# Layer 3: the 3x3 convolution of the last 32 channels moved from TensorE to ScalarE and GpSimd

## The chip, the cores and the metric

The kernel runs on one core of a Trainium2 chip. The metric is the device time of one execution, in microseconds (us); the figure for a kernel is the median of its runs. A profiled execution gives the trace that the views below are taken from. In them, PE is TensorE, DVE is VectorE, ACT is ScalarE, POOL is GpSimd, and SP is the engine that issues most DMAs.

## What is computed

Four layers run one after another on x, four images of 48 channels and 256 x 256 pixels in float32. Each adds its result to its input, which it first normalises over groups of channels. Layer 0 is a gated network with a depthwise 3x3 convolution and an 8x8 frequency filter, layers 1 and 2 are scans with a convolution along rows and columns, and layer 3, which the change touches, is this (shortened):

```python
y = jnp.einsum('oc,bchw->bohw', w_in, x)               # 48 -> 288 channels
yp = ...                                               # 8 x 8 patches of y
f = jnp.fft.rfft2(yp) * fft_mask[None]
yp = jnp.fft.irfft2(f, s=(P, P))
y = lax.conv_general_dilated(y, w_dw, ..., feature_group_count=288)   # 3x3, each channel by itself
x1, x2 = jnp.split(y, 2, axis=1)                       # 144 and 144 channels
g = jax.nn.gelu(x1, approximate=False) * x2
return jnp.einsum('oc,bchw->bohw', w_out, g)           # 144 -> 48 channels
```

## The kernel before

Images are worked on in two pairs. In layer 3 (`layer3`) each pair is cut into 32 strips of 8 rows (`RB`); a strip and one tail row at the end of the pair make 33 steps, 66 in all. The 3x3 convolution needs the rows above and below, so a step's convolved rows lie one row higher than its strip, and `lines` copies the last two rows of the strip before on ScalarE.

One step goes as follows. `fetch` brings a strip from memory (a DMA on SP's queue). `ready` normalises it into the tile `u` (eight ACTIVATEs, line 1043). `turn` transposes it on TensorE (line 1058), `wave` takes it to the frequency domain (line 1072), `spectra` applies the 48 to 288 matrix (line 1093), and DVE applies the mask while it copies the result out of PSUM (lines 1096 and 1101). `pixels` brings four blocks of channels back to pixels (line 1131); ACT and DVE copy them out (line 1051; letters such as "AD" say which engine takes which half) into the tiles `z_a0`, `z_a1`, `z_b0`, `z_b1`. The 144 channels of each half of the network are 128 and 16. a0 and b0 hold the first 128 of x1 for the first and the second image, a1 and b1 the first 128 of x2. The remaining 16 channels of each half, 32 in all, of both images make the fifth group, m: `pixels_rest` (line 1150) brings it to `z_m`, 64 partitions at a time, the upper and the lower half of the partitions in turn for odd and even steps.

The convolution is done in two ways. On TensorE, `taps` (line 1167) and `lower_taps` (line 1183) do nine products with a diagonal 32 x 32 matrix for each block of 32 channels and two rows, accumulated in PSUM. On DVE, `begin` makes the first product on ACT (line 1222) and queues eight taps (line 1227, a scalar times a shifted tile plus the accumulator, all in SBUF) in the list `due`; these do the upper four rows of b0 and b1. A final gelu on ACT (line 1229) and a product on DVE (line 1231) close them.

TensorE's share is cut into units, run two at a time in `together`, one for each lane: lane l does blocks 2l and 2l+1, and the taps of both lanes alternate. There are units a0 and a1 for both lanes, b (the lower four rows of b0 and b1) for both lanes, and m for one lane a step. Two steps make fourteen units, that is seven rounds of `together`. During a round `together` also takes five items from `due`. After a unit its result leaves PSUM: a0 by a gelu on ACT (`curve`, line 1204), a1 by a product on DVE (`gate`, line 1210), b by a gelu on ACT and a product on DVE (lines 1193 and 1194), m by both (lines 1204 and 1210) into `g_m`.

`store` drains what is left in `due` for a step and calls `mixed`: the projection from 144 to 48 channels on TensorE (lines 1249 and 1259), into two PSUM tiles `po`; DVE adds the strip of the input (line 1272), and SP writes it out. Its last products read `g_m`.

Layer 3 is scheduled by hand: each engine's queue holds its instructions in the order in which the program writes them, within the loop at the end of `layer3`, which writes two steps per pass. PSUM has four tiles of two banks (`ps_w`) for everything, taken in turn.

Of the kernel before, what the change touches and what calls it, by code (L numbers as in the profile page):

```python
# [33 lines left out]
class Net:  # L34
# [901 lines left out]
    def layer3(self, x, scs):  # L936
# [11 lines left out]
        with ExitStack() as st:  # L948
# [54 lines left out]
            for half in range(2):  # L1003
                lo = half * HD
                nc.sync.dma_start(wd[:, half, :], self.a["L3_w_dw"][lo : lo + NM, :])
                for l in range(2):
                    at = 64 * l + 32 * half
                    nc.sync.dma_start(wd[at : at + 2 * NR, 2, :], self.a["L3_w_dw_r"][half])
            diag = wp.tile([128, 3, 9, 32], F32, name="diag")
            none = wp.tile([128, 1], F32, name="none")  # L1010
            nc.gpsimd.memset(none, 0.0)

# [14 lines left out]

            zt = {}
            for g in ("a0", "a1", "b0", "b1", "m"):
                zt[g] = (wz if g == "m" else wp).tile([128, RB + 2, WP], F32, name=f"z_{g}", tag=f"z_{g}")  # L1030
                nc.gpsimd.memset(zt[g][:, :, 0:1], 0.0)
                nc.gpsimd.memset(zt[g][:, :, WP - 1 : WP], 0.0)
            gated = {g: wz.tile([128, 4, MM], F32, name=f"g_{g}", tag=f"g_{g}") for g in "ab"}
            gated["m"] = wz.tile([128, 1, MM], F32, name="g_m", tag="g_m")

# [69 lines left out]

            def lines(step, g):

                n, at, old = (64, 64 * odd(step), 64 - 64 * odd(step)) if g == "m" else (128, 0, 0)  # L1110
                t, above = zt[g][at : at + n], zt[g][old : old + n]
                if step[1] == 0:
                    nc.gpsimd.memset(t[:, 0:2, 1 : W + 1], 0.0)
                else:
                    nc.scalar.copy(t[:, 0:2, 1 : W + 1], above[:, RB : RB + 2, 1 : W + 1])
                if tail(step):
                    nc.gpsimd.memset(t[:, 2, 1 : W + 1], 0.0)
                return t
# [22 lines left out]
            def pixels_rest(step, eng):  # L1141

                t = lines(step, "m")
                if tail(step):
                    return
                pp = ps_w.tile([128, 2, 8, 64], F32, name="pp", tag="w")
                for q in range(NQ):
                    for l in range(2):
                        f = slice(64 * l, 64 * l + 64)
                        nc.tensor.matmul(  # L1150
                            pp[64 * (q % 2) : 64 * (q % 2) + 64, l, q // 2, :],
                            zr[f, q, :], self.inv1[f, :], start=True, stop=True,
                        )
                to = t[:, 2 : RB + 2, 1 : W + 1].rearrange("p h (q j l w) -> p j l q h w", j=2, l=2, w=8)
                for j in range(2):
                    for l in range(2):
                        copy(eng[l], to[:, j, l], pp[64 * j : 64 * j + 64, l].rearrange("p q (h w) -> p q h w", w=8))

            def taps(step, g, half, blocks, pd):
                for t in range(9):
                    for j in range(1 if tail(step) else 4):
                        n = 1 if tail(step) else R2
                        for i, k in enumerate(blocks):
                            s = slice(32 * k, 32 * k + 32)
                            nc.tensor.matmul(  # L1167
                                pd[32 * j : 32 * j + 32, i, 0:n, :], diag[s, 2 if g == "m" else half, t, :],
                                zt[g][s, R2 * j + t // 3 : R2 * j + t // 3 + n, t % 3 : t % 3 + W],
                                start=(t == 0), stop=(t == 8),  # L1170
                            )
                    yield True
# [43 lines left out]
            def begin(step, half):  # L1216
# [16 lines left out]

                due.extend(((step, half), lambda t=t: tap(t)) for t in range(1, 9))

            def drain(step, half):

                while any(key == (step, half) for key, _ in due):
                    due.pop(0)[1]()

            def mixed(step):
# [2 lines left out]
                h0 = s * RB - 1  # L1244
                js, n = (range(1), 1) if tail(step) else (range(4), R2)
                pos = [ps_w.tile([128, 2, R2, W], F32, name="po", tag="w") for _ in js[::2]]
                part = whole.pop(step)
                for j in js[:2]:
                    nc.tensor.matmul(  # L1249
                        pos[0][64:128, j, 0:n, :], wo_b, part[:, R2 * j : R2 * j + n, :], start=True, stop=False  # L1250
# [1 line left out]
                for i in range(5):  # L1252
                    for j in js:
                        for b in range(2):
                            if b and j < 2 and i < 4:
                                continue
                            r = slice(32 * j, 32 * j + 32)
                            src = gated["m"][r, 0] if i == 4 else gated["ab"[b]][r, i]
                            nc.tensor.matmul(  # L1259
                                pos[j // 2][64 * b : 64 * b + 64, j % 2, 0:n, :], wo[r, i + b * (i == 4), :],  # L1260
                                src[:, 0 : n * W].rearrange("p (r w) -> p r w", w=W),
                                start=(i == 0), stop=(i == 4),
                            )
                for j0, po in zip(js[::2], pos):
# [20 lines left out]
            out, units = set(), [[], []]  # L1285
            for n, step in enumerate(steps):
                for l in range(2):
                    units[l] += [(step, img) for img in ("a0", "a1", "b") + (("m",) if n % 2 == l else ())]
            assert len(units[0]) == len(units[1])
            waiting = [None, None]  # L1290

            def unit(l, step, img):
# [4 lines left out]
                if img == "b":  # L1297
                    if not tail(step):
                        pd = ps_w.tile([128, 2, R2, W], F32, name="pd", tag="w")
                        yield from lower_taps(step, blocks, pd)  # L1300
                else:
                    pd = ps_w.tile([128, 2, R2, W], F32, name="pd", tag="w")
                    half = int(img[1]) if img[0] == "a" else 0
                    yield from taps(step, img, half, blocks, pd)
                if img == "a0":
                    waiting[l] = curve(step, pd)
                    return
                assert n == 0 or steps[n - 1] in out
                if img == "a1":
                    gate(step, "a", 2 * l, waiting[l], pd)  # L1310
                elif img == "m":
                    gate(step, img, 0, curve(step, pd[:, 0:1]), pd[:, 1:2])
                elif pd is not None:
                    lower_gate(2 * l, pd)

            def together(k, aside=None):


                going = [unit(l, *units[l][k]) for l in range(2)]
                for t in range(9):  # L1320
                    for g in list(going):
                        if next(g, None) is None:
                            going.remove(g)
                    if t == 1 and aside is not None:
                        aside()
                    if due and (t + 1) * 5 // 9 > t * 5 // 9:
                        due.pop(0)[1]()
                for g in going:
                    assert next(g, None) is None
# [38 lines left out]
            def lower(n, half, q0, eng):  # L1368
# [3 lines left out]
                if q0:  # L1372
                    begin(steps[n], half)

            fetch(steps[1])
            scale(1)
            ready(0)
            turn(0, "AD")
            wave(0, "AD")
            spectra(0, 0)  # L1380
            for k in range(3):
                for t in range(9):
                    nc.vector.tensor_scalar(diag[:, k, t, :], eye, wd[:, k, t : t + 1], None, ALU.mult)
            ready(1)
            k = 0
            for n in range(0, S, 2):
                o = n + 1
                pixels(steps[n], "a0", 0, "AD")
                pixels(steps[n], "a0", 8, "AD")
                spectra(n, 1, slice(0, 2))  # L1390
                lower(n, 0, 0, "AA")
                spectra(n, 1, slice(2, 4))
                lower(n, 0, 8, "AA")
                spectra(n, 1, slice(4, None))
                together(k)

                pixels(steps[n], "a1", 0, "DD")
                pixels(steps[n], "a1", 8, "DD")
                store(n - 1)
                if fresh(n + 2):  # L1400
                    fetch(steps[n + 2])
                turn(o, "AA")
                together(k + 1)

                wave(o, "AA")
                lower(n, 1, 0, "AA")
                lower(n, 1, 8, "AA")
                spectra(o, 0)
                together(k + 2)

                pixels(steps[o], "a0", 0, "AD")
                pixels(steps[o], "a0", 8, "AD")
                pixels_rest(steps[n], "AD")
                spectra(o, 1, slice(0, 3))
                lower(o, 0, 0, "AA")
                spectra(o, 1, slice(3, None))
                together(k + 3)

                pixels(steps[o], "a1", 0, "DD")
                pixels(steps[o], "a1", 8, "AD")  # L1420
                store(n)
                if fresh(n + 3):
                    fetch(steps[n + 3])
                lower(o, 0, 8, "AA")
                together(k + 4, lambda: ready(n + 2))

                turn(n + 2, "AA")
                lower(o, 1, 0, "DD")
                lower(o, 1, 8, "AD")
                wave(n + 2, "A", (0,))  # L1430
                together(k + 5)

                pixels_rest(steps[o], "AD")
                wave(n + 2, "A", (8,))
                spectra(n + 2, 0)
                together(k + 6, lambda: ready(n + 3))
                k += 7
            store(S - 1)


# [116 lines left out]
```

## Time and profile before

| | |
|---|---|
| median of 3 runs | 12905.28 us (12900.96 to 12907.49) |
| profiled execution | 12935.81 us, span 12934.0 us |
| layer 3 in the span | from about 8560 us to the end, some 4370 us |
| busy in the whole span | PE 94%, DVE 58%, ACT 28%, POOL 10% |
| mean granted TensorE clock | 0.985 of full speed |
| tap matmuls of layer 3 in the trace | z_a 37152 records, z_b 18432, z_m 9288 (two records for each matmul) |

Lines of the trace give a start in us from the span's start, a length in us, the engine, the line of the kernel, the operation, the tile written and the tiles read, and the shape (partitions x elements). "x4" is a run of four such instructions merged. Square brackets hold the idle time of the engine just before, and what ended it. In a table by stretch each engine's entry is its busy time and, in brackets, its instructions; the last three columns are the granted clock, the DMA share and GB/s. A matmul's end is modelled, so matmuls that run beside each other in different parts of the array each show some 0.6 us, while a round of 288 records takes 9.75 us.

### The profile page before, as it was taken

The numbers are of one execution on the slowest core, as the hardware profiler recorded it, in microseconds if no ns is written. First come the engines' busy times: TensorE is split into PE (matmuls) and PEld (weight loads), VectorE is DVE, ScalarE is ACT, GpSimd is POOL, SyncE is SP. The second block draws the span as 40 slices with busy tenths as digits, with TensorE's granted clock in tenths as the row PEclk, the third lists the DMA queues.
The fourth block names the chain that finished last, engine by engine and source line by source line (L and its number), as shares of the span: only waits on it lengthen the run. The fifth ranks groups of instructions, "written<-read, shape, count | busy, mean of one in ns | idle before, by whom it ended". The sixth has DMA issues, their size and how long they took to land.

```text
span 12934.0 us, 426071 instructions
## 1 busy us (share of the span) xinstructions
PE 12148.3 (94%) x199864; PEld 7975.0 (62%) x199864; DVE 7459.6 (58%) x11269; ACT 3608.4 (28%) x4015; POOL 1333.8 (10%) x977
## 2 busy tenths in 40 slices
PE   2999999999999999999999999989999999999999
PEld 0333333335777777777777777766666666666666
DVE  6777777774333334663333335566666666676666
ACT  1444444442223200002233000023333333333333
POOL 0010010100000001540000004510000000000000
PEclk9999999999999999999999999999999999999999
DMA  7222222225765776987756877931111111111111
GB/s 176 56 56 56 56 58 56 58 53 96 155 138 152 172 155 134 225 199 157 145 144 155 173 153 178 229 61 28 23 28 28 28 26 26 28 23 28 28 28 21
DMA packets 1170350, 1224.62 MB, mean 95 GB/s; under 512 B 1027668, under 2 KB 1031756, under 8 KB 1107724
## 3 DMA queue, kind: packets, MB, share of 16 engines
q1 hardware_dynamic: 1066052, 623.85, 26.2%
q0 software_dynamic: 87488, 445.55, 11.9%
q10 hardware_dynamic: 15048, 127.96, 5.4%
q8 instruction: 1566, 25.66, 0.9%
q14 instruction: 196, 1.61, 0.0%
HBM read 699.79 MB, written 497.42 MB: 93 GB/s over the span
## 4 chain that ended last, share of the span: by engine, by line
PE 87%; ACT 5%; DVE 3%; issue 3%; DMA 2%; SPq 0%; POOL 0%; ACTq 0%; DVEq 0%; POOLq 0%
PE acc L682 40%; PE pd L1167 12%; PE pd L313 9%; PE pd L1183 5%; PE pp L1131 4%; PE pz L1093 4%; PE po L1259 2%; PE ph L290 2%; PE ph L282 1%; DMA gx<-in_x 1%; PE py L387 1%; PE po L457 1%; PE py L394 1%; PE po L1249 1%; PE pf L1072 1%
## 5 line engine op out<-in xcount | busy, mean ns | idle before, releaser
L682 PE MATMUL acc<-line,w_down 96*96 96x256 f32 x12240 | 2660.9, 379 | 14.5 <-ACT line L780 4.9
L682 PEld LDWEIGHTS acc<-line,w_down 96*96 96x96 f32 x12240 | 1989.1, 163 | 671.5 <-DVE line L824 11.5
L1167 PE MATMUL pd<-z_a,diag 32*32 32x512 f32 x37152 | 1622.2, 596 | 42.2 <-issue 32.3
L313 PE MATMUL pd<-main,diag 32*32 32x512 f32 x36864 | 1426.8, 622 | 66.6 <-issue 63.6
L682 PE MATMUL acc<-line,w_right 96*96 96x256 f32 x6120 | 1339.9, 380 | 23.4 <-DVE line L862 18.2
L1227 DVE SCALAR_TENSOR_TENSOR acc<-z_b,wd,acc 128x1024 f32<-128x1024 f32 (+1 forms) x1056 | 1326.1, 1258 | 60.8 <-ACT acc L1222 33.5
L682 PE MATMUL acc<-line,w_left 96*96 96x256 f32 x6120 | 1339.2, 379 | 9.6 <-DVE line L903 7.6
L350 DVE SCALAR_TENSOR_TENSOR acc<-rest,wd,acc 128x1024 f32<-128x1024 f32 x1024 | 1256.7, 1285 | 127.2 <-ACT acc L344 127.0
L682 PEld LDWEIGHTS acc<-line,w_right 96*96 96x96 f32 x6120 | 997.1, 163 | 354.4 <-DVE line L862 19.0
L682 PEld LDWEIGHTS acc<-line,w_left 96*96 96x96 f32 x6120 | 996.0, 163 | 339.0 <-DVE line L903 16.1
L1167 PEld LDWEIGHTS pd<-z_a,diag 32*32 32x32 f32 x37152 | 857.4, 103 | 524.3 <-issue 233.2
L313 PEld LDWEIGHTS pd<-main,diag 32*32 32x32 f32 x36864 | 505.0, 105 | 779.8 <-issue 666.6
L865 DVE SCALAR_TENSOR_TENSOR line<-acc,b_right,in 96x256 f32<-96x256 f32 x1020 | 489.6, 480 | 850.7 <-PE acc L682 850.7
L789 DVE TENSOR_TENSOR line<-acc,in 96x256 f32<-96x256 f32 x1020 | 428.9, 421 | 920.2 <-PE acc L682 914.3
L824 DVE SCALAR_TENSOR_TENSOR line<-acc,b_down,in 96x256 f32<-96x256 f32 x992 | 476.1, 480 | 830.3 <-PE acc L682 823.5
L1183 PE MATMUL pd<-z_b,diag 32*32 32x512 f32 x18432 | 933.0, 597 | 2.6 <-issue 1.9
L903 DVE SCALAR_TENSOR_TENSOR line<-acc,b_left,in 96x256 f32<-96x256 f32 x992 | 475.8, 480 | 530.9 <-PE acc L682 530.9
L124 ACT ACTIVATE nrm<-nrm 96x2 f32<-96x2 f32 (+1 forms) x7 | 1.4, 203 | 2796.2 <-DVE nrm L123 1421.9
L913 POOL TENSOR_TENSOR blk<-blk,line 96x1024 f32<-96x1024 f32 x248 | 705.3, 2872 | 608.1 <-DVE line L903 608.1
L1096 DVE TENSOR_TENSOR z<-pz,mask 128x768 f32<-128x768 f32 (+2 forms) x640 | 627.5, 1003 | 218.4 <-PE pz L1093 215.8
L831 ACT COPY blk<-line 96x1024 f32<-96x1024 f32 (+2 forms) x264 | 479.7, 1888 | 922.9 <-DVE line L824 760.6
L1131 PEld LDWEIGHTS pp<-c_inv,z 64*64 64x64 f32 x32768 | 528.9, 136 | 252.3 <-issue 140.9
(167 smaller groups left out, 12915.3 us busy)
## 6 DMA issues: line engine op xcount, KB each, us to landing
blk<-x ACTq DMA_DIRECT2D x64, 1536.0 KB, 18.1
in<-x SPq DMA_DIRECT2D x248, 384.0 KB, 11.2
dn<-line POOLq DMA_DIRECT2D x124, 768.0 KB, 9.5
rt<-line POOLq DMA_DIRECT2D x124, 768.0 KB, 9.9
in<-rt SPq DMA_DIRECT2D x124, 768.0 KB, 12.8
in<-dn SPq DMA_DIRECT2D x120, 768.0 KB, 6.9
in<-up SPq DMA_DIRECT2D x240, 384.0 KB, 11.7
up<-blk POOLq DMA_DIRECT2D x56, 1536.0 KB, 14.5
```

The costliest lines, as they stand in the source:

```text
L313: nc.tensor.matmul(pd[32 * j : 32 * j + 32, i], diag[s, t, :], z[s, R2 * j + t // 3 : R2 * j + t // 3 + R2, t % 3 : t % 3 + W], start=(t = ...
L350: nc.vector.scalar_tensor_tensor(to, at(t, r), wd[:, 1, t : t + 1], to, ALU.mult, ALU.add)
L682: self.nc.tensor.matmul(acc, w[:, t, :], carry[:, :, t : t + m], start=(t == 0), stop=(t == 2))
L831: nc.scalar.copy(blk[:, :, e, lo:hi, k // 2 : k // 2 + RH], inner(ln[:, e::2])[..., lo:hi].rearrange("p h i w -> p i w h"),)
L865: nc.vector.scalar_tensor_tensor(blocks(inner(line)), blocks(acc), br, new, ALU.add, ALU.add)
L913: (nc.vector if w0 == 0 else nc.gpsimd).tensor_tensor(part, part, inner(ln[:, f::2])[..., lo:hi].rearrange("p w i h -> p i h w"), ALU.add)
L1093: nc.tensor.matmul(pz[:, b, q, :], xf[s, q0 + q, :], wi[s, NM * k : NM * k + m], start=True, stop=True)
L1096: nc.vector.tensor_tensor(zs[k][:, q0 : q0 + n].rearrange("p q b c -> p b q c"), pz[:, :, :, 0:NM], mask[:, :, :, NM * k : NM * k + NM].to ...
L1131: nc.tensor.matmul(pp[64 * c : 64 * c + 64, l, q, :], z[f, q0 + q, b, 64 * c : 64 * c + 64], self.inv1[f, :], start=True, stop=True,)
L1167: nc.tensor.matmul(pd[32 * j : 32 * j + 32, i, 0:n, :], diag[s, 2 if g == "m" else half, t, :], zt[g][s, R2 * j + t // 3 : R2 * j + t // 3 ...
L1183: nc.tensor.matmul(pd[to, i], diag[s, half, t, :], zt[f"b{half}"][s, R2 * j + t // 3 : R2 * j + t // 3 + R2, t % 3 : t % 3 + W], start=(t ...
L1227: nc.vector.scalar_tensor_tensor(acc, at(t), wd[:, half, t : t + 1], acc, ALU.mult, ALU.add)
```

## The change

The m units are taken out of TensorE. `z_m` is now split by rows instead of by steps: partitions 0 to 63 hold the strip's upper part and partitions 64 to 127 the lower, so that all 128 partitions each give four convolved rows. `pixels_rest` therefore writes four pieces of four rows and four of six rows.

`narrow` queues 18 products in the list `coming`: nine taps by two halves of two rows. A product is one ACTIVATE on ScalarE that multiplies a shifted view of `z_m` by the channel's weight. For the first tap it writes the accumulator `acc_m`; for the others it writes the tile `part`, which has two buffers, and GpSimd adds `part` to `acc_m`. `together` calls `product` at given taps: seven times in the round of a1, seven in the round of b, four in the round of a0 of the next step. `ready` stands in the round of b, at its fifth tap. `gate_few` is called at the seventh tap of that a0 round: it issues what is left of the products, and `narrow_gate`, two gelus on ScalarE and four products on VectorE. `mixed` reads the result from `acc_m` instead of `g_m`.

The loop now writes one step per pass, with three rounds of `together`, and six items of `due` are taken in a round. `diag` has two groups instead of three. Cut to its core:

```diff
@@ lines
-                n, at, old = (64, 64 * odd(step), 64 - 64 * odd(step)) if g == "m" else (128, 0, 0)
-                t, above = zt[g][at : at + n], zt[g][old : old + n]
+                t = zt[g]
+                t, last = (t, t[:, RB:]) if g != "m" else (t[0:64], t[64:128, HR:])
@@ pixels_rest
-                to = t[:, 2 : RB + 2, 1 : W + 1].rearrange("p h (q j l w) -> p j l q h w", j=2, l=2, w=8)
-                for j in range(2):
-                    for l in range(2):
-                        copy(eng[l], to[:, j, l], pp[64 * j : 64 * j + 64, l].rearrange("p q (h w) -> p q h w", w=8))
+                for h0, h1, lo, to in ((0, HR, 2, t), (HR - 2, RB, 0, zt["m"][64:128])):
+                    to = to[:, lo : HR + 2, 1 : W + 1].rearrange("p h (q j l w) -> p j l q h w", j=2, l=2, w=8)
+                    for j in range(2):
+                        for l in range(2):
+                            copy(
+                                eng[l], to[:, j, l],
+                                pp[64 * j : 64 * j + 64, l].rearrange("p q (h w) -> p q h w", w=8)[:, :, h0:h1],
+                            )
+            def narrow(step):
+                n, rows = (64, 1) if tail(step) else (128, HR)
+                at = lambda t: zt["m"][0:n, t // 3 : t // 3 + rows, t % 3 : t % 3 + W]
+                acc = mid.tile([128, HR, W], F32, name="acc_m", tag="acc_m")
+                few[step] = acc
+                acc = acc[0:n, 0:rows]
+                half = lambda ap, r: ap[:, R2 * r : min(R2 * r + R2, rows)]
+                def tap(t, r):
+                    if t == 0:
+                        nc.scalar.activation(half(acc, r), half(at(0), r), AF.Identity, bias=none[0:n], scale=wd[0:n, 2, 0:1])
+                        return
+                    part = mid.tile([128, R2, W], F32, name="part", tag="part", bufs=2)[0:n, 0 : min(R2, rows)]
+                    nc.scalar.activation(part, half(at(t), r), AF.Identity, bias=none[0:n], scale=wd[0:n, 2, t : t + 1])
+                    nc.gpsimd.tensor_tensor(half(acc, r), half(acc, r), part, ALU.add)
+                halves = range(1 if tail(step) else 2)
+                coming.extend(lambda t=t, r=r: tap(t, r) for t in range(9) for r in halves)
+            def product(last=False):
+                while coming:
+                    coming.pop(0)()
+                    if not last:
+                        return
+            def narrow_gate(step):
+                gl, acc = io.tile([128, HR, W], F32, name="gl", tag="gl"), few[step]
+                for j0 in (0,) if tail(step) else (0, 2):
+                    x1, x2 = slice(32 * j0, 32 * j0 + 32), slice(32 * j0 + 32, 32 * j0 + 64)
+                    rows = 1 if tail(step) else HR
+                    nc.scalar.activation(gl[x2, 0:rows], acc[x1, 0:rows], AF.Gelu)
+                    for j in range(1 if tail(step) else 2):
+                        to, r = slice(32 * (j0 + j), 32 * (j0 + j) + 32), slice(R2 * j, min(R2 * j + R2, rows))
+                        nc.vector.tensor_tensor(acc[to, r], gl[x2, r], acc[x2, r], ALU.mult)
@@ units and together
-                    units[l] += [(step, img) for img in ("a0", "a1", "b") + (("m",) if n % 2 == l else ())]
+                    units[l] += [(step, img) for img in ("a0", "a1", "b")]
-                    if t == 1 and aside is not None:
-                        aside()
-                    if due and (t + 1) * 5 // 9 > t * 5 // 9:
+                    if t in aside:
+                        aside[t]()
+                    if due and (t + 1) * 6 // 9 > t * 6 // 9:
                         due.pop(0)[1]()
@@ the loop, one step per pass (the two-step pass of before is in the listing above)
+            def gate_few(n):
+                if n >= 0:
+                    product(True)
+                    narrow_gate(steps[n])
+            for n, step in enumerate(steps):
+                pixels(step, "a0", 0, "AD")
+                pixels(step, "a0", 8, "AD")
                 spectra(n, 1, slice(0, 2))
                 lower(n, 0, 0, "AA")
                 spectra(n, 1, slice(2, 4))
                 lower(n, 0, 8, "AA")
                 spectra(n, 1, slice(4, None))
+                together(3 * n, {t: product for t in range(4)} | {6: lambda: gate_few(n - 1)})
+                pixels(step, "a1", 0, "DD")
+                pixels(step, "a1", 8, "AD")
+                pixels_rest(step, "AD")
                 store(n - 1)
+                narrow(step)
                 if fresh(n + 2):
                     fetch(steps[n + 2])
+                turn(n + 1, "AA")
+                together(3 * n + 1, {t: product for t in range(2, 9)})
+                wave(n + 1, "AA")
                 lower(n, 1, 0, "AA")
                 lower(n, 1, 8, "AA")
+                spectra(n + 1, 0)
+                together(3 * n + 2, {t: product for t in range(8) if t != 4} | {4: lambda: ready(n + 2)})
+            gate_few(S - 1)
             store(S - 1)
```

## The prediction

> **What bounds the kernel now.** I read the page's busy slices and its chain first: layer 3 is the last third, from 8560 us on, and the chain runs on TensorE (PE) nearly throughout. Then busy time by stretch:
>
> ```profile
> core 0: us, PE busy (x) PEld busy (x) DVE busy (x) ACT busy (x) POOL busy (x), PEclk, DMA share, GB/s
> 8700.00:12750.00 4050.00, 3839.25 (x114165) 2622.74 (x114166) 2754.20 (x3277) 1480.43 (x2134) 4.19 (x10) 0.99 0.15 27
> ```
>
> PE is busy 95%, VectorE (DVE) 68%, ScalarE (ACT) 37%, GpSimd (POOL) never. The waits of PE in layer 3 say how rarely it is held: mostly by nothing the profile shows, and only some tens of us by copies. So the stage lasts as long as PE's list. Next the chain in order of time, for one step:
>
> ```profile
> 9625.02 9.68 PE pd L1167 x272
> 9634.70 2.02 PE pp L1131 x128
> 9636.72 1.86 PE po L1249 x4
> 9638.58 4.50 PE po L1259 x62
> ```
>
> One round of `together` (two lanes, 288 matmul records) takes 9.75 us; 4370 us of layer 3 (8560 to the end) over 64 full steps and two short ones make 66.5 us a step (3.5 rounds, and transforms between), 62 without half a round. Then the order of DVE and ACT in that step, since the change lives in their queues (start, length, engine, line):
>
> ```profile
> 9625.01 1.24 ACT L1222 ACTIVATE acc<-z_b,none,wd 128x1024 f32<-128x1024 f32 x1
> 9634.40 1.94 ACT L1204 ACTIVATE gl<-pd 128x1024 f32<-128x1024 f32 x2 [8.15 <-PE pd L1167]
> 9626.40 1.27 DVE L1227 SCALAR_TENSOR_TENSOR acc<-z_b,wd,acc 128x1024 f32<-128x1024 f32 x1
> 9627.71 1.22 DVE L1231 TENSOR_TENSOR acc<-acc,acc 128x1024 f32<-128x1024 f32 x1
> 9628.85 5.24 DVE L1227 SCALAR_TENSOR_TENSOR acc<-z_b,wd,acc 128x1024 f32<-128x1024 f32 x4
> 9636.88 2.48 DVE L1051 COPY z_a<-pp 128x512 f32<-128x512 f32 x4 [2.79 <-ACT z_a L1115]
> ```
>
> ACT idles 8 us in a round: room for products. DVE fills the same round with `tap` instructions back to back, 1.20 us apart, both tensor operands in SBUF. Would POOL additions run beside them? Layers 0 to 2 show both engines together:
>
> ```profile
> 278.11 7.25 DVE L350 SCALAR_TENSOR_TENSOR acc<-rest,wd,acc 128x1024 f32<-128x1024 f32 x6
> 280.04 5.80 POOL L274 COPY rest<-rest 128x512 f32<-128x512 f32 x1 [10.11 <-ACT rest L296]
> 296.69 1.87 POOL L274 COPY main<-main 128x1024 f32<-128x1024 f32 x1 [10.86 <-PE pd L313]
> 297.69 1.95 DVE L350 SCALAR_TENSOR_TENSOR acc<-rest,wd,acc 128x1024 f32<-128x1024 f32 x1
> 5743.13 5.67 POOL L913 TENSOR_TENSOR blk<-blk,line 96x1024 f32<-96x1024 f32 x2 [8.11 <-DVE line L903]
> 5746.16 2.76 DVE L913 TENSOR_TENSOR blk<-blk,line 96x64 f32<-96x64 f32 x1
> ```
>
> The POOL copy (median 0.62) took 5.80: it sat until the whole train of DVE taps was over. The DVE sum of 96x64 (0.25 at its least) took 2.76: it sat until the POOL sum ended. Either blocks the other when both read two SBUF operands (a POOL copy too). The 541 DVE instructions of line 903 beside POOL sums, which read PSUM and SBUF, kept their 0.48 us.
>
> **Part by part, per step** (64 full steps, 2 tails).
>
> *Removed.* The m units: 72 matmuls of 32x512 (two records each; 9288 in all), half a round: 9.75/2 = -4.9 us of PE, on the path. Their gelu (0.60 ACT) and gate (0.69 DVE) go too, and nine `diag` instructions once, hidden. Order and PSUM tiles of the other units stay; each step now has the list of the former even steps, plus `pixels_rest` ahead of `store`.
>
> *Rest copies.* Four of 64x512 (0.65 ACT, 0.69 DVE, each waiting for the last, 2.7 us in all) become eight of 256 or 384 columns, about 8 x 0.5 = 4 us. They lie beside the output projection (1.86 + 4.50 us): nothing; without that cover 1.3.
>
> *Products.* 18 ACTIVATEs of 128x512. Rows: 112x256 at 0.588, 128x1024 at 1.231, so 0.80 each, 0.75 apart: 13.5 us. Two gelus of 32x1024 at 1.01 (row of 64x1024). ACT gets from 25 to some 41 us of 62: fits in sum.
>
> *Additions.* 16 on POOL, 128x512. Nearest row 96x1024 at 2.87; the two copy forms (1.045 and 0.616) give 0.19 fixed; (2.87 - 0.19)/2 + 0.19 = 1.52 us, 24 us a step. Bounds: 1.43 (half the row) and 2.87. The Trainium skill, "GPSIMD Engine Reference", Performance versus the Vector engine, gives 4497 ns for such a sum of 2048 columns; a quarter is an estimate of 1.12 us, and with it the stalls below would shrink by some 3 us a step, to about 13,120.
>
> *The port.* DVE needs it for 16 taps x 1.2, one product 1.2 and four narrow gates x 0.6 = 23 us, POOL 24: 47 of 62 us. In sum it fits; the order decides. `part` has two buffers, so ACT's third product waits for POOL's first addition, and behind ACT's product stand its gelus out of PSUM, whose four tiles hold PE. Times below run from the first tap matmul of a round.
>
> Round a0 (four products, then `narrow_gate` in the middle of DVE's taps). ACT's first product ends at 2.0. DVE starts taps at 1.4. Before the narrow gelus the port must serve four additions (6.1); DVE's four taps and one product ahead of the narrow gates take 6.0. If POOL gets in after two taps (at the 0.04 us gap ahead of L1231, as at 296.69), additions end at 10.0, the gelus at 12.0, DVE's rest at 13.6, its gates and two last taps at 18.4. If DVE's train goes first (as at 280.04), additions end at 13.5, gelus at 15.5, DVE at 19.1. Before, DVE was at its a1 copies at 11.9 (the row at 9636.88). These now end at 19.8 to 20.5; the second `po` tile needs their PSUM, wanted at 9.7 + 2.1 + 1.2 + 1.9 = 14.9. Stall 4.9 to 5.6; I take 5.0. Without the lock: 0.3.
>
> Round a1 (seven products, five additions; four taps). DVE's taps end near 5, the additions near 12.5, the last product near 10.3; wanted by then are only DVE's gates (one operand in PSUM) and ACT's copies at 11. Nothing. If this cover goes, 4.
>
> Round b (seven products and additions; six taps; `ready`, eight ACTIVATEs of 0.59, after the fourth product). ACT starts at -1.5, after L1222. Two additions end at 2.3; then a train of six taps (7.2) and further additions take turns. Whichever is first, additions three to five and the taps end at 2.3 + 7.2 + 4.6 = 14.1, and only then has product seven a buffer: it ends at 14.9, the first lower gelu at 15.9, its gate on DVE at 17.1 where it was at 11.7 (9676.27 + 1.2). PE wants that tile for the next spectra: stall about 5; 4.5 taken, as PE has two pixel groups ahead. Without the lock, product seven ends at 9.9: 0.2.
>
> *Clock.* PE's granted clock after an idle window:
>
> ```profile
> 9389.72:9393.12 3.40, 1.48 (x98) 1.34 (x94) 0.00 (x0) 2.70 (x4) 0.00 (x0) 1.00 0.02 5
> 9393.14:9396.54 3.40, 3.40 (x66) 3.28 (x58) 0.26 (x1) 2.23 (x3) 0.00 (x0) 0.50 0.02 5
> ```
>
> 1.9 us idle in 3.4 brought 3.4 us at half clock, 1.7 us of work lost. Two stalls per step: 0 to 3.4; I take one, 1.7, since after round b PE runs beside a DVE-bound stretch. The Trainium skill, "TensorE: Matmul & The Clock Gate", Why this matters for your kernels, asks for idle gaps over about 3 us; this row shows 1.9 enough, and by the page the stalls, broken by short groups, would often cost nothing here, some 110 us less.
>
> `fetch` now comes every step, one round and a half ahead of `ready`; it lands in 7.7 us and has some 24 (a round of 9.75, the 10 us up to the next, four taps of 1.1). SP carries the same transfers, POOL has no DMA in this layer: nothing.
>
> **Sum.** -4.9 + 5.0 + 4.5 + 1.7 = +6.3 us x 64 = +403. The profiled execution (span 12934.0, 12935.8 with its ends) is 30 us above the median of the runs; the difference is the same on either: 12,905 + 403 = 13,310. With stalls of 3 and 3 and no lost clock +1.1 a step, with 6, 6 and 3.4 +10.5: own range 12,975 to 13,580.
>
> **Rivals.**
> Hidden (faster): the port is shared finely enough that additions run between taps, as the throughput (47 of 62 us) allows. -4.9 + 0.5 = -4.4 x 64 = -280: 12,625. For it: ACT's and POOL's idle; against: the 5.80 and 2.76 rows. It decides when the stalls of rounds a0 and b together stay under 4.9 us a step.
> Half: products run ahead of taps by ACT's slack and half of both stalls vanishes: -4.9 + 2.5 + 2.25 + 0.85 = +0.7 x 64 = +45: 12,950, either sign, 12,780 to 13,100.
> Spill: round a1 stalls as well, 4.5 and another clock window: +6.2 x 64 more: 13,700.
> That PE's matmuls aren't removed is excluded by the diff.
>
> **Chances.** Forecast 0.52, hidden 0.20, half 0.20 (0.07 faster, 0.03 same, 0.10 slower), spill 0.08. A change under 0.2% a measurement of this kernel can't tell from none. Faster 0.27, same 0.03, slower 0.70. The range leaves out half of hidden and spill: 12,620 to 13,620.
>
> **What would show it.** Tap matmuls fewer by 9288; POOL about 1020 sums in layer 3, some far above 1.5 us, and DVE taps at 1.27 or 2 to 3 us; ACT products waiting for POOL; the chain in layer 3 passing through POOL, ACT gelus and DVE; PE idle ahead of the second `po` tile and the spectra; clock below 0.98. Wrong if POOL sums and DVE taps overlap at their plain lengths, or PE's waits stay near 200 us in layer 3.

## The result, and the profile after

The changed kernel takes 13,192.4 us (median of 4 runs, 13,170.3 to 13,219.6) against 12,905.8 before (median of 4 by then): a ratio of 1.0224 (95% interval 1.0202 to 1.0245), 287 us slower. The profiled execution has a span of 13,168.5 us. Layers 0 to 2 are the same; layer 3 went from 4374 to 4609 us there.

The table by stretch, in the middle of layer 3, changed kernel (columns as before):

```profile
8700.00:12950.00 4250.00, 3721.96 (x105179) 2582.78 (x105180) 3371.74 (x3443) 2473.22 (x3498) 1707.05 (x962) 0.94 0.15 25
```

PE's share falls from 95% to 88% though it has less to do, its clock from 0.99 to 0.94, and DVE rises from 68% to 79% though little was added to its list. What PE waited for in layer 3 (us in total, times, longest):

```profile
PE pz L1093 <- DVE g_b L1198: 225.7, 62, 4.2
PE pp L1150 <- ACT gl L1208: 118.1, 62, 2.0
PE po L1292 <- ACT gl L1208: 40.3, 61, 0.7
```

Once a step each: the spectra ahead of round a0 wait for the lower gate of round b, and the rest pixels and the first `po` tile, after round a0, wait for a gelu on ACT. Before, none of the three was among PE's waits in layer 3; the longest in total was "issue", waiting for nothing that the profile shows, and the longest for a named engine was small:

```profile
PE pp L1131 <- issue: 67.3, 61, 2.7
PE pz L1093 <- ACT xf L1051: 18.5, 28, 0.8
```

One step in order of time, DVE, then POOL, then ACT in round b (its last tap matmul ends at 9451.74):

```profile
9443.96 12.50 DVE L1231 SCALAR_TENSOR_TENSOR acc<-z_b,wd,acc 128x1024 f32<-128x1024 f32 x6
9456.49 2.37 DVE L1198 TENSOR_TENSOR g_b<-gl,pd 64x1024 f32<-64x1024 f32 x2
9441.57 7.03 POOL L1258 TENSOR_TENSOR acc_m<-acc_m,part 128x512 f32<-128x512 f32 x4 [6.30 <-ACT part L1257]
9449.67 5.70 POOL L1258 TENSOR_TENSOR acc_m<-acc_m,part 128x512 f32<-128x512 f32 x3 [1.07 <-ACT part L1257]
9451.82 1.92 ACT L1197 ACTIVATE gl<-pd 64x1024 f32<-64x1024 f32 x2
```

Six taps take 12.50 us, 2.1 each; in the same round before, five took 6.56:

```profile
9667.50 6.56 DVE L1227 SCALAR_TENSOR_TENSOR acc<-z_b,wd,acc 128x1024 f32<-128x1024 f32 x5
```

ACT's gelus start at 9451.82, 0.1 us after the round: ACT is on time. DVE's gate starts 4.7 us after the round, behind its own taps. The stretch that follows, up to the next round, runs at a mean granted clock of 0.78:

```profile
9451.74:9467.36 15.62, 11.62 (x321) 10.66 (x321) 13.21 (x16) 6.59 (x11) 3.63 (x2) 0.78 0.01 3
```

In round a0 the chain in order of time reads:

```profile
9469.44 8.45 POOL acc_m L1258 x4
9477.89 0.02 issue
9477.91 1.07 ACT gl L1274
9478.98 0.02 issue
9479.00 0.68 DVE acc_m L1277
```

Four additions take 8.45 us and the narrow gelu waits for them; then the four narrow gates, and only when they have freed a `gl` buffer the second `curve` (9481.89), and `po` starts at 9482.97, 5.9 us after the round's end at 9477.11. The last gate, that `curve` and `po`:

```profile
9481.09 0.70 DVE acc_m L1277
9481.89 1.03 ACT gl L1208
9482.97 1.93 PE po L1292 x4
```

At the 1.28 us that an addition takes alone, the four additions would take an estimated 5.1, 3.3 less. Lengths of one instruction (ns, min/median/max) of taps and additions:

```profile
L1231 DVE SCALAR_TENSOR_TENSOR acc<-z_b,wd,acc x1056: 472/2172/2386, 8553.8 to 13158.2; 128x1024 f32<-128x1024 f32 x172, 128x256 f32<-128x256 f32 x4
L1258 POOL TENSOR_TENSOR acc_m<-acc_m,part x1040: 715/2112/2352, 8575.3 to 13155.1; 128x512 f32<-128x512 f32 x171, 64x256 f32<-64x256 f32 x3
```

Of the 1021 taps that start after 8700 us 562 take over 1.5 us, most of them 2.2, and 605 of 1040 additions take over 1.6 us; alone either takes 1.28. A tap beside an addition loses 0.9 us to it, and the addition 1.0 to the tap. "The port" below means whatever path into SBUF the two take in turns.

### The profile page after: what moved, and what is told of

Its sections match the earlier page's. It is cut to its first block, busy times and chain, and to the rows that moved or that the text cites. A ratio compares the mean times of both kernels' runs of the same rounds, so it can differ in the third digit from the quotient of the medians.

```text
span 13168.5 us, 410466 instructions
## 1 busy us (share of the span) xinstructions
PE 12021.7 (91%) x190576; PEld 7936.0 (60%) x190576; DVE 8137.4 (62%) x11452; ACT 4693.1 (36%) x5505; POOL 3192.8 (24%) x2017
## 4 chain that ended last, share of the span: by engine, by line
PE 72%; DVE 12%; ACT 6%; POOL 4%; issue 3%; DMA 2%; SPq 0%; ACTq 0%; DVEq 0%; POOLq 0%
PE acc L682 40%; PE pd L313 9%; DVE acc L1231 6%; PE pd L1171 5%; POOL acc_m L1258 4%; PE pz L1093 3%; PE pp L1131 3%; PE po L1304 2%; DVE z L1096 2%; PE ph L290 2%; DVE acc_m L1277 1%; PE ph L282 1%; DMA gx<-in_x 1%; PE py L387 1%; PE pf L1072 1%
## 5 line engine op out<-in xcount | busy, mean ns | idle before, releaser
L1258 POOL TENSOR_TENSOR acc_m<-acc_m,part 128x512 f32<-128x512 f32 (+1 forms) x1040 | 1852.5, 1808 | 2760.7 <-ACT part L1257 2759.6
L682 PEld LDWEIGHTS acc<-line,w_down 96*96 96x96 f32 x12240 | 1989.2, 163 | 671.5 <-DVE line L824 11.5
L1231 DVE SCALAR_TENSOR_TENSOR acc<-z_b,wd,acc 128x1024 f32<-128x1024 f32 (+1 forms) x1056 | 1864.0, 1765 | 41.7 <-ACT acc L1226 13.6
L1171 PE MATMUL pd<-z_a,diag 32*32 32x512 f32 x37152 | 1324.0, 597 | 54.2 <-issue 38.6
L1171 PEld LDWEIGHTS pd<-z_a,diag 32*32 32x32 f32 x37152 | 762.0, 103 | 518.7 <-issue 205.1
L1093 PE MATMUL pz<-wi,xf 48*128 48x128 f32 x8192 | 711.6, 330 | 242.0 <-DVE g_b L1198 225.7
L1257 ACT ACTIVATE part<-z_m,none,wd 128x512 f32<-128x512 f32 (+1 forms) x1040 | 805.3, 803 | 344.8 <-POOL acc_m L1258 344.8
## 6 DMA issues: line engine op xcount, KB each, us to landing
in<-x SPq DMA_DIRECT2D x248, 384.0 KB, 11.4
```

The source lines that it names most:

```text
L682: self.nc.tensor.matmul(acc, w[:, t, :], carry[:, :, t : t + m], start=(t == 0), stop=(t == 2))
L1093: nc.tensor.matmul(pz[:, b, q, :], xf[s, q0 + q, :], wi[s, NM * k : NM * k + m], start=True, stop=True)
L1171: nc.tensor.matmul(pd[32 * j : 32 * j + 32, i, 0:n, :], diag[s, half, t, :], zt[g][s, R2 * j + t // 3 : R2 * j + t // 3 + n, t % 3 : t % 3 ...
L1231: nc.vector.scalar_tensor_tensor(acc, at(t), wd[:, half, t : t + 1], acc, ALU.mult, ALU.add)
L1257: nc.scalar.activation(part, half(at(t), r), AF.Identity, bias=none[0:n], scale=wd[0:n, 2, t : t + 1])
L1258: nc.gpsimd.tensor_tensor(half(acc, r), half(acc, r), part, ALU.add)
```

## The experiments

All but one are edits of the changed kernel; the one headed "And those two moved as well" is shown against the version just before it. Ratios are to the kernel before on the same chip.

**Without the additions.**

```diff
-                    nc.gpsimd.tensor_tensor(half(acc, r), half(acc, r), part, ALU.add)
```

> The changed kernel without GpSimd's 16 additions a step (they are left out, so acc_m holds the first product alone); products, narrow gates, copies and order stay. Theory A (port: a VectorE tap and a GpSimd addition take turns, and VectorE's queue runs late): taps go from 2.18 back to 1.27 us, the half-clock windows go from 97 to about 20, time 12,560 to 12,680 us (before less half a round a step, 312 us). Theory B (ScalarE's own load: 18 products of 0.8 us stand ahead of its gelus): the products are all still there, so most of the loss stays and the time is 12,950 us or more.

12,630 us, ratio 0.9765 (0.9749 to 0.9781). The taps:

```profile
L1231 DVE SCALAR_TENSOR_TENSOR acc<-z_b,wd,acc x1056: 473/1285/1300, 8551.5 to 12601.9; 128x1024 f32<-128x1024 f32 x172, 128x256 f32<-128x256 f32 x4
```

None is above 1.30, and the three waits of PE are gone, with 18 products still on ACT. 0.9765 is 303 us under before (310 by the medians of this comparison, 12,630 and 12,940), against the 312 us of half a round a step. The 9 us between lie within the interval, so ACT's own load costs next to nothing, and the loss comes with the additions. Theory B falls. Medians over 62 to 64 steps, from the last tap matmul of one round to the first of the next, show where (us):

| | changed | without additions | half additions | between | between, more |
|---|---|---|---|---|---|
| round b to a0 | 15.6 | 9.5 | 9.9 | 11.6 | 9.8 |
| round a0 to a1 | 14.8 | 11.5 | 12.6 | 11.3 | 11.4 |
| round a1 to b | 10.2 | 10.2 | 10.2 | 10.3 | 10.6 |
| three rounds, sum of medians | 30.2 | 30.7 | 30.9 | 30.9 | 31.1 |

6.1 us a step are lost after round b, 3.3 after round a0, nothing after a1.

**Three buffers for the products.**

```diff
-                    part = mid.tile([128, R2, W], F32, name="part", tag="part", bufs=2)...
+                    part = mid.tile([128, R2, W], F32, name="part", tag="part", bufs=3)...
```

> The changed kernel with three part buffers instead of two (eye shares acc_m's memory to make room). Theory A: the port is as busy as before, VectorE's taps stay at 2.18 us where an addition is under way; the time stays within 0.5%: 13,120 to 13,250 us. Theory C (ScalarE, held by GpSimd through the two part buffers, is what makes the gelus late): ScalarE's 345 us of waiting for part falls by half or more and the time falls by 100 us or more, below 13,090 us.

13,187 us, ratio 1.0194 (1.0179 to 1.0209) beside 1.0224 (1.0202 to 1.0245) of the change: the intervals touch. To make room, `eye`, which is needed once, shares the memory of `acc_m`. ACT's wait for `part`, 344.8 us in the change, nearly goes:

```profile
ACT part L1257 <- POOL acc_m L1258: 45.8, 77, 1.4
```

But the stretches after b and a0 are 15.8 and 14.8 us, as in the change. ACT held through `part` isn't the path; theory C falls.

**Additions over half of the columns.**

```diff
-                    nc.gpsimd.tensor_tensor(half(acc, r), half(acc, r), part, ALU.add)
+                    nc.gpsimd.tensor_tensor(half(acc, r)[:, 0:1], half(acc, r)[:, 0:1], part[:, 0:1], ALU.add)
```

> The changed kernel with each addition over one of its two rows, 256 of 512 columns (half of the sums is left out); number, order and waits stay. Theory A with a lock held for the whole instruction: an addition alone goes from 1.27 to about 0.73 us, a tap beside one from 2.18 to about 1.65, and about half to two thirds of the loss against the kernel without additions goes: 12,780 to 12,980 us. If the price were one fixed turn for each instruction, whatever its length, taps stay above 2 us and the time above 13,100 us.

12,715 us, ratio 0.9831 (0.9816 to 0.9847). Additions alone take 0.73 us, and 450 of the 1024 taps that start after 8700 us are above 1.5, mostly at 1.64:

```profile
L1231 DVE SCALAR_TENSOR_TENSOR acc<-z_b,wd,acc x1056: 473/1285/1860, 8578.9 to 12706.2; 128x1024 f32<-128x1024 f32 x172, 128x256 f32<-128x256 f32 x4
```

The tap's wait follows the addition's length: 0.35 for 0.73, 0.90 for 1.28, some 0.38 less than all of it both times. The lengths are as expected; the time is 65 us below the range given. The loss isn't in proportion: with taps at 1.64, the stretch after round b is 9.9 us long instead of 15.6. It may be that DVE's queue has slack for the first tenths of a us of each tap and none for the rest; no run shows it by itself.

**The m group's taps on VectorE.**

```diff
-                    nc.scalar.activation(part, half(at(t), r), AF.Identity, bias=none[0:n], scale=wd[0:n, 2, t : t + 1])
-                    nc.gpsimd.tensor_tensor(half(acc, r), half(acc, r), part, ALU.add)
+                    nc.vector.scalar_tensor_tensor(acc, at(t), wd[0:n, 2, t : t + 1], acc, ALU.mult, ALU.add)
...
-                    if due and (t + 1) * 6 // 9 > t * 6 // 9:
+                    if due and (t + 1) * 8 // 9 > t * 8 // 9:
```

> The m group's eight later taps as VectorE taps of 128x1024 in the same list due (eight items a round instead of six); ScalarE makes the first product only, GpSimd adds nothing. VectorE has 8 x 1.2 = 9.6 us a step more of its own work, some 57 of 62 us in all. Theory A: this costs VectorE less than 16 turns at the port of 0.9 us each did, and nothing waits for ScalarE: 12,650 to 12,850 us, faster than before. Theory D (VectorE is simply too full; any work given to it makes its queue late): 12,950 us or more.

13,365 us, ratio 1.0336 (1.0317 to 1.0355): a miss for theory A as I had applied it, and in the range of theory D. No tap is above 1.30, but there are half as many again. D can't explain the change itself, though: the kernel without additions gives DVE the same list as the change and is fast. ACT's and PE's waits in layer 3 name the path:

```profile
ACT acc L1233 <- DVE acc L1231: 721.1, 64, 11.8
PE pp L1150 <- ACT gl L1208: 305.9, 63, 5.1
PE pz L1093 <- DVE g_b L1198: 193.3, 62, 3.3
```

With eight items a round the last tap of b0 falls at the end of round a0; its gelu (L1233) stands in ACT's queue ahead of `curve`, and PE waits for `curve`. So a queue late by its own work hurts in the same two places as one late by the port. How much of the 721 us a better order of `due` would give back wasn't tried.

**TensorE kept busy in the stall.**

```diff
+                for k in range(idle):                  # idle = 8 for the second half of a0
+                    c, l = k % 2, k // 2 % 2
+                    f = slice(64 * l, 64 * l + 64)
+                    nc.tensor.matmul(pp[64 * c : 64 * c + 64, l]..., nought[f], zs[0][f, 0:2]..., start=True, stop=True)
```

> The changed kernel with eight products of 64x64 by 512 columns with zero weights on TensorE in each step, into the second pp tile of a0 ahead of the real ones (which overwrite them): TensorE works some 1.7 us in the stall ahead of the spectra instead of idling, nothing else is touched. If the half clock after an idle window is a real part of the loss: half-clock time in layer 3 falls from 505 us to under 350 us and the time by 50 to 110 us, to 13,080 to 13,140 us. If the stall itself is the whole loss (VectorE's lateness sets the end whatever the clock): 13,170 to 13,230 us.

13,152 us, ratio 1.0178 (1.0158 to 1.0199), beside 1.0224 of the change: 40 us less by the medians and some 60 by the ratios, whose intervals don't meet; the time lies between the two ranges given. PE's wait for the gate falls, as it must:

```profile
PE pz L1095 <- DVE g_b L1207: 129.9, 60, 2.5
```

The half-clock time of layer 3, summed from the granted clock, is 396 us instead of 505 (61 before the change, 68 without additions; from 8600 us on, without the last window, in which the kernel ends): less of a fall than expected, which was to under 350. Half of 109 us is 55 us of work, and the time fell by about as much: useless work in a stall made the kernel faster. That fits the clock being a part of the loss, by half of 505 - 61 at most 222 us, but with neither range met it doesn't prove the share; the idle time of PE, 581 us in layer 3 against 226, is the other part.

**Copies in place of additions.**

```diff
-                    nc.gpsimd.tensor_tensor(half(acc, r), half(acc, r), part, ALU.add)
+                    nc.gpsimd.tensor_copy(half(acc, r), part)
```

> The changed kernel with a GpSimd copy of part to acc_m in place of each addition (the sums are left out): one SBUF operand is read instead of two. In the trace of before a copy took 0.62 us alone and once sat 5.80 us behind a train of taps. If copies and taps exclude each other too: copies of 0.62 alone and over 1.3 beside taps, taps of some 1.5, time 12,680 to 12,900 us; if copies are starved by whole trains: copies of 4 us and more, ScalarE held through part, time above 13,000 us; if one operand doesn't exclude: 12,600 to 12,660 us.

12,639 us, ratio 0.9779 (0.9756 to 0.9802), where no additions at all give 0.9765. Copies take 0.61 us alone and up to 1.67 beside taps, taps 1.51 beside copies: a GpSimd copy that reads one SBUF operand is enough for the two to exclude each other, but with turns this short DVE is in time again. The lengths are those expected for exclusion, the time is not: it lies in the range given for none, 12,600 to 12,660. No copy waited for a whole train.

**Products between the rounds.**

```diff
                 pixels(step, "a0", 8, "AD")
+                products(3)
                 spectra(n, 1, slice(0, 2))
                 lower(n, 0, 0, "AA")
+                products(2)
...
-                together(3 * n, {t: product for t in range(4)} | {6: lambda: gate_few(n - 1)})
+                together(3 * n, {4: lambda: gate_few(n - 1)})
...
                 narrow(step)
+                products(4)
...
-                together(3 * n + 1, {t: product for t in range(2, 9)})
+                together(3 * n + 1, {t: product for t in range(6, 9)})
...
                 lower(n, 1, 0, "AA")
+                products(2)
                 lower(n, 1, 8, "AA")
+                products(2)
...
-                together(3 * n + 2, {t: product for t in range(8) if t != 4} | {4: lambda: ready(n + 2)})
+                together(3 * n + 2, {4: lambda: ready(n + 2), 5: product, 6: product})
```

> The changed kernel with the same 18 products, 16 additions and narrow gates, but most of them issued between the rounds, where VectorE copies out of PSUM and leaves the port: four after narrow, three late in round a1, two and two around the lower pixels, two in round b, three and two ahead of round a0; narrow gates at the fifth tap of round a0. Theory A (the meeting of taps and additions is the loss, not the work itself): taps beside an addition fall from some two thirds to under a third, time 12,660 to 12,820 us, faster than before. If GpSimd's and ScalarE's amount of work were the loss: above 13,000 us.

12,818 us, ratio 0.9917 (0.99 to 0.9934): the same work, 0.8% faster than before the change. 326 of the 1018 taps that start after 8700 us still take over 1.3 us, beside an addition. After round a0 nothing is lost any more; after round b 2.1 us are, and its six taps take

```profile
9440.13 10.11 DVE L1231 SCALAR_TENSOR_TENSOR acc<-z_b,wd,acc 128x1024 f32<-128x1024 f32 x6
```

because the additions of the two products left in round b, and one ahead of it, meet them. (At 12,818 us the time is at the upper end of the range given.)

**And those two moved as well.**

```diff
-                wave(n + 1, "AA")
+                wave(n + 1, "A", (0,))
+                products(2)
+                wave(n + 1, "A", (8,))
...
-                together(3 * n + 2, {4: lambda: ready(n + 2), 5: product, 6: product})
+                together(3 * n + 2, {4: lambda: ready(n + 2)})
```

> As the kernel with the products between the rounds, but with the two products of round b moved ahead of the second wave copy, where VectorE waits for TensorE. Theory A: in round b no addition meets a tap but the first; six taps take about 8 us instead of 10.1, the stretch from round b to a0 falls from 11.6 us to under 10.3, and the time by 1.3 us or more a step: 12,650 to 12,760 us. If what holds that stretch were ScalarE's or GpSimd's work and not the meeting: 12,800 us or more.

12,704 us, ratio 0.9833 (0.9814 to 0.9852). This version beats both kernels, and comes within 0.7% of the kernel without additions. The additions that ran only beside DVE instructions with an operand in PSUM, 523 of them, took 1.28 us, the longest 1.31. In one step round b reads

```profile
9432.56 9.03 DVE L1231 SCALAR_TENSOR_TENSOR acc<-z_b,wd,acc 128x1024 f32<-128x1024 f32 x6
```

where about 8 us were expected: its first two taps still meet an addition. The stretch after it is 9.8 us (median), down from 15.6 in the change. PE's longest waits in layer 3 have no name again, as before the change.

**Taps in two.**

```diff
-                    nc.vector.scalar_tensor_tensor(acc, at(t), wd[:, half, t : t + 1], acc, ALU.mult, ALU.add)
+                    for r in range(0, rows, R2):
+                        a = acc[:, r : min(r + R2, rows)]
+                        nc.vector.scalar_tensor_tensor(
+                            a, at(t)[:, r : min(r + R2, rows)], wd[:, half, t : t + 1], a, ALU.mult, ALU.add
+                        )
```

> The changed kernel with each of VectorE's taps of 128x1024 as two of 128x512, one for each pair of rows, so that the next instruction doesn't need the result of the one just before it (as the taps of layer 0 do, which follow each other with an overlap of 0.07 us, where those of layer 3 stand 0.03 us apart). Theory E (GpSimd gets the port only in such a gap): no turns any more; additions that come during a train end after it, 3 us and longer, as the copy of 5.80 us in layer 0 did; the halves stay at 0.68 us but for the first of a train; ScalarE waits for part longer than 345 us; time 13,050 to 13,400 us. If turns are taken after each instruction whatever the gap: halves of 1.5 us, additions of 1.6, VectorE twice as late, 13,400 us or more.

13,336 us, ratio 1.0319 (1.0302 to 1.0336). The halves overlap by 0.08 us as the taps of layer 0 do, and 63 additions, one a step, are above 3 us:

```profile
L1262 POOL TENSOR_TENSOR acc_m<-acc_m,part x1040: 714/1552/6732, 8584.1 to 13322.3; 128x512 f32<-128x512 f32 x171, 64x256 f32<-64x256 f32 x3
```

The first addition of round a1 does wait for the train (4.18 us in one step, while eight halves take 5.38). But 453 others take over 1.6 us, nearly all 1.6 to 1.8, in turns with trains that overlap just as much, and 500 halves take over 1.3 us instead of 0.74. ScalarE waits 296 us for part, not longer than the 345. So the time is in the range given and the reason for it is not: the gap alone doesn't decide who gets the port, and the question stays open. That taps in two make a slower kernel is what the run shows.

## Why the prediction was right or wrong

*The gain.* -4.9 us a step: right. Without additions the kernel is 303 us under before, where 312 had been worked out.

*The mechanism.* Right in the main: taps and additions exclude each other, DVE's queue runs late, and PE waits for PSUM after rounds b and a0 and not after a1. Removing the additions, shortening them, or moving them out of the taps' way brings the gain back in that order of size.

The path inside each round was partly another than the prediction had. In round b it let product seven wait for a `part` buffer, ACT's gelu start at 14.9 us from the round's first matmul and the gate end at 17.1. In the step above (first matmul at 9441.99) the gelu starts at 9.8, on time, and the gate ends at 15.7 because DVE is busy with its own six taps; with a third `part` buffer nothing is gained. In round a0 the additions and the narrow gelu did hold things up as forecast, but what came late for PE was `curve` on ACT, not DVE's a1 copies (below). There no run separates the turns at the port from the additions' plain time ahead of the narrow gelu; that the four took an estimated 3.3 us longer than alone, about what the stretch after a0 lost, speaks for the turns.

*The sizes.* Forecast +403 us, measured +287. The loss is 6.1 + 3.3 - 0.5 (the rounds) = 8.9 us a step instead of 5.0 + 4.5 + 1.7 = 11.2.

- The clock term ("0 to 3.4; I take one, 1.7") was too small: 444 us more at half clock are up to 222 us of work, 3.5 a step, where 1.7 was taken.
- The stalls were too large: PE's three named waits are 384 us, 6.0 a step, for 9.5. The term that was mis-sized is the addition, taken at 1.52 from the row of 96x1024; it is 1.28, and an addition and a tap together take 2.2, not 1.5 + 1.2. The estimate of 1.12, from the Trainium skill's page "GPSIMD Engine Reference", Performance versus the Vector engine, was nearer than the row. The other way, the taps of layer 3 stand 1.31 apart, not 1.20, which is the spacing in the layer 0 line: four in 5.24 us, in a line that the prediction shows.
- After round a0 I had the second `po` tile, held by DVE's a1 copies, as what is late. It was `curve`, for the second of which the narrow gates, with the same two `gl` buffers, made a wait that I had not seen; 118 + 40 us.
- The clock and the stalls are not separate: what a stretch shows, 6.1 us after round b, holds both.
- Part of the closeness of the sum is luck: stalls 3.5 us too large and a clock term up to 1.8 too small worked against each other.

*The rivals.* "Hidden" needed stalls under 4.9 us a step; the last order of the products comes near its 12,625 us, the change's, with 6.0 us of waits, doesn't. "Half" falls by the time, 13,192 against at most 13,100, but its stalls of 4.75 us a step are nearer to the measured 6.0 than the forecast's 9.5; the clock, up to 3.5 a step, can be the rest. "Spill" falls with the table: round a1 loses nothing.

*What I missed.* That the same 24 (measured: 20) us of additions fit between the rounds, where DVE reads PSUM and the two don't hold each other up. The profile of before had it: DVE's instructions on PSUM ran beside POOL sums at their plain 0.48 us.

## What to carry to other kernels

An engine that is idle isn't free if it and a busy one hold each other up, as VectorE's taps and GpSimd's additions do here: look in the trace for one place where both read SBUF at once, compare the lengths there with the shortest, and then count which queues stand behind the longer ones. If the two must share, issue the one's work where the other reads PSUM. Here that order alone took the ratio from 1.0224 (1.0202 to 1.0245) to 0.9833 (0.9814 to 0.9852), with the same instructions.

## What the runs showed of the hardware

- A VectorE instruction with two SBUF operands and a GpSimd addition take turns: 2.18 and 2.26 us instead of 1.28 each, in a pitch of 2.2, with 605 of 1040 additions concerned. A GpSimd copy with one SBUF operand does it too (1.51 for the tap). A VectorE instruction with an operand in PSUM does not: 523 additions beside such instructions alone took 1.28 us in the last order. The Trainium skill, "SBUF — State Buffer", SBUF: two separate sides, says that the pair of ports is locked for the whole instruction; the waits here grow with the other's length, as that would have it, but a tap's are some 0.38 us shorter than the addition (0.90 for 1.28, 0.35 for 0.73).
- Whether GpSimd gets a turn or sits out a train differs: at most 2.35 us in the change, 5.8 once in layer 0, 3.2 to 6.7 once a step with the taps in two. What decides it isn't settled.
- Useless products in a stall of up to 4.2 us a step (the wait fell by 96 us in all) went with 109 us less at half clock and a kernel some 40 us faster by the medians.
